# Three transposed contexts read from memory by columns, and the sums of self attention in another buffer

## The chip, the cores and the metric

The kernel runs on one core of one Trainium2 chip. The metric is the device time of one execution in microseconds (us). The core has five engines that run their own instruction streams in order and wait for each other by semaphores: TensorE (PE in the profile, with its weight loads as PEld), VectorE (DVE), ScalarE (ACT), GpSimd (POOL) and SyncE (SP). Transfers between memory and the on-chip buffers are issued by an engine's instruction stream, here SP's or ACT's, and carried out by 16 DMA engines.

## The reference

One decoder layer in fp32 on 4 entries of 512 tokens by 512 features, 16 heads of 32 features:

```python
x = x + self_attention(layernorm(x))      # causal; q, k, v and o projections with biases
x = x + cross_attention(layernorm(x), ctx, ctx)   # no projections; causal, masked scores are -10000
x = x + ffn(layernorm(x))                 # relu(x Wup) Wdown + sum(top-2 softmax) * (x Wexpert)
```

In cross attention the context is both key and value, without a projection. The scores contract over a head's features, so TensorE needs the context with its features on the partitions (512 features as 4 chunks of 128 partitions, by 512 tokens); the values need it with its tokens on the partitions, as it lies in memory.

## The kernel before

The four entries are worked on one after the other, but overlapped: while the engines do the softmax of one stage, TensorE is filled with matmuls of another (the feed-forward of entry b beside the maxima of self attention of entry b+1, for example). The order of PE, DVE, ACT and POOL is written out by hand and is the order of the program text. SP's order is set by the framework. Each engine takes its instructions strictly in that order, the issue of a DMA included.

For each entry b the stages are:

1. maxima of self attention (`with_maxima`): score matmuls (`sm_s`, L286), a copy by ACT (`s_s`, L297), a mask by POOL and a maximum by DVE, with the previous entry's feed-forward or this entry's projections as filler;
2. scores, exponentials and values of self attention (`attend`): `sc_s`, ACT's exponentials, `pv_s`. For the head groups g = 0, 1, 2 the sums of the exponentials are gathered in a buffer `self.sums[g]` of one full activation tile, taken from the buffers `ck_t` (g even) and `beh_t` (g odd);
3. the output projection (`pm_o`, L687). Between its matmuls stand the side steps: the transposes that make the transposed context `ckT` (from `cv`, by `columns`: 8 transposes `tp_c` on PE into PSUM and one copy by ACT, done twice for an entry) and the transposes that make the next entry's `xnT` (`tp_a`). After its second chunk `behind` lets DVE scan `ckT` from the back (L672);
4. query and key projection of the next entry, then maxima (`sm_c`) and `attend` of cross attention, which read `ckT`;
5. value projection of the next entry (`pm_v`), the back transposes `tp_x`, the layernorm, and the transposes `tp_f` with ACT's copy `fT` that open the feed-forward.

All activation tiles have one buffer for each tag, so `ck_t` holds the sums of self attention first and the transposed context after them. `load_cv` reads the context of entry b+1 on SP right after cross attention of entry b, when `cv` is free. `load_x(0)` puts two of its four loads on ACT's queue; all other loads are SP's, until one store at the end.

In the program before, the first entry's ACT instructions are: two loads, the copies of `xnT`, then the query and key outputs `kT` and `qT` (L604, L607).

A DMA of this program carries its completion in one of eight semaphores, given out in rotation over all DMAs in the framework's order. A DMA whose semaphore is still in use by an earlier one waits for that one before it is issued.

Of the kernel before, what the change touches and what calls it, by code (L numbers as in the profile page):

```python
# [9 lines left out]
F32 = mybir.dt.float32  # L10
# [8 lines left out]
P = 128  # L19
# [7 lines left out]
def decoder_layer(  # L27
# [21 lines left out]
    nc = tc.nc  # L49
    B, S, D = x.shape  # L50
# [3 lines left out]
    NC = D // P  # L54
# [5 lines left out]
    act = ctx.enter_context(tc.tile_pool(name="act", bufs=1))  # L60
# [17 lines left out]
    def load_cv(b):  # L78
        cv = act.tile([P, NT, D], F32, tag="cv", name=f"cv_{b}")
        src = ctx_in[b].rearrange("(t p) d -> p t d", p=P)  # L80
        for t in range(NT):
            nc.sync.dma_start(out=cv[:, t, :], in_=src[:, t, :])
        return cv

    def load_w(ap, name, parts=1):
        w = const.tile([P, NC, ap.shape[-1]], F32, tag=name, name=name)
# [175 lines left out]
    class Attention:  # L262
# [114 lines left out]
        def scores(self, pieces):  # L377


            at, N = [], 0  # L380
            for g, j in pieces:
                at.append(N)
                N += S - j * P
            name = f"{self.name}_{pieces[0][0]}_{pieces[0][1]}"
            scs = [pair(f"sc_{name}_{n}") for n in range(2)]
            for (g, j), c in zip(pieces, at):
                for r in range(HG):
                    h = slice(r * HD, (r + 1) * HD)
                    nc.tensor.matmul(  # L389
                        scs[r // 2][:, r % 2, c : c + S - j * P],  # L390
                        lhsT=self.k_t[h, g, j * P : (j + 1) * P],
                        rhs=self.q_t[h, g, j * P :],
                        start=(c == 0),
                        stop=False,
                        skip_group_check=(len(pieces) > 1),
                    )
            for (g, j), c in zip(pieces, at):
                for r in range(HG):
                    h = slice(r * HD, (r + 1) * HD)
                    nc.tensor.matmul(  # L400
                        scs[r // 2][:, r % 2, c : c + S - j * P],
                        lhsT=onesb[h, :],
                        rhs=self.mrow[g][h, j * P :],
                        start=False,
                        stop=True,
                        skip_group_check=(len(pieces) > 1),
                    )
            g, j = pieces[0]
            pts = []
            if j == 0 and g in self.added:  # L410

                self.sums[g] = act.tile(
                    [P, 2, 2, S],
                    F32,
                    tag="v" if self.cross else ("ck_t", "beh_t")[g % 2],
                    name=f"sum_{name}",
                )
            for n in range(2):
                if j == 0 and g in self.added:
                    pt = self.sums[g][:, n]  # L420
                else:
                    pt = work.tile([P, 2, S], F32, tag="pt", name=f"pt_{name}_{n}", bufs=6)
                nc.scalar.activation(pt, scs[n], AF.Exp)  # L423

                if len(pieces) == 1:
                    diagonal = pt[:, :, :P].unsqueeze(2)
                elif j == pieces[1][1]:
                    diagonal = pt.rearrange("p u (k q) -> p u k q", k=2)[:, :, :, :P]
                else:
                    diagonal = pt[:, :, : 2 * P].rearrange("p u (k q) -> p u k q", k=2)  # L430
                nc.gpsimd.affine_select(  # L431
                    out=diagonal,
                    in_=diagonal,
                    compare_op=ALU.is_ge,
                    fill=0.0,
                    base=0,
                    pattern=[[0, 2], [0, len(pieces)], [1, P]],
                    channel_multiplier=-1,
                )
                pts.append(pt)  # L440
            return [(g, j, c, pts) for (g, j), c in zip(pieces, at)]
# [144 lines left out]
    def add_bias(e):  # L586
        for t in range(NT):
            nc.gpsimd.tensor_tensor(e.x[:, t, :], e.x[:, t, :], bo_sb, ALU.add)
# [67 lines left out]
    def context(e):  # L656

        b = e.b
        e.cv = cvs.pop(b)
        e.ck_t = act.tile([P, NC, S], F32, tag="ck_t", name=f"ckT_{b}")  # L660

        def one(t):
            columns([e.cv[:, t, :], e.cv[:, t + 1, :]], e.ck_t, t, pair(f"tp_c{b}_{t}"))

        return [(lambda t=t: one(t)) for t in (0, 2)]
# [15 lines left out]
    def out_projection(e, a, sides):  # L681

        b = e.b
        pms = [pair(f"pm_o{b}_{n}") for n in range(2)]
        for c in range(NC):
            for t in range(NT):
                nc.tensor.matmul(  # L687
                    pms[t // 2][:, t % 2, :],
                    lhsT=a.out[:, c, t * P : (t + 1) * P],
                    rhs=wo_sb[:, c, :],  # L690
                    start=(c == 0),
                    stop=(c == NC - 1),
                )
            if c < NC - 1:
                run(sides[c::3])
            if c == 1:
                for g in range(NC):
                    behind(e, g)

        def add(t):  # L700
            xi = e.x[:, t, :]
            nc.vector.tensor_tensor(xi, pms[t // 2][:, t % 2, :], xi, ALU.add)

        made, norms = layernorms(lambda t: e.x[:, t, :], f"q{b}", add)
        run(norms)
        return made
# [147 lines left out]
    def run(steps):  # L854
        for step in steps:
            for _ in step() or ():
                pass
# [89 lines left out]
    with tc.manual_schedule(engines=BY_HAND):  # L947
        e, norms, turns = norm_in(0, x0)
        keep_warm("warm", 12)
        run(norms)  # L950
        run(turns)
        nc.gpsimd.tensor_scalar(bqs_sb, bq_sb, SCALE, None, ALU.mult)
        nc.vector.tensor_reduce(
            fold, ident.rearrange("p (c e) -> p e c", e=HD), axis=AX.X, op=ALU.add
        )
        add_bias(e)
        between_self = query_key(e) + value(e)
        skip, between_cross, ahead = 4, [], []
        for b in range(B):
            more = b + 1 < B  # L960
            sa = Attention(e.q_t, e.k_t, e.v, False, f"s{b}")
            norms, turns = [], []
            if more:
                after, norms, turns = norm_in(b + 1)
            late = with_maxima(between_self, sa, skip, norms)
            if b == B - 1:
                e.x = load_x(b)
            attend(sa, late)
            if b > 0:
                add_bias(e)  # L970
            made = out_projection(e, sa, context(e) + turns)
            steps = (query_key(after) if more else []) + between_cross
            run(steps[:2])
            norm_cross(e, made, 0)
            run(steps[2:3])
            norm_cross(e, made, 2)
            ca = Attention(e.cq_t, e.ck_t, e.cv, True, f"c{b}")
            ca.e, ca.out = e, e.beh_t
            late = with_maxima(steps[3:], ca)
            if b + 2 < B:  # L980
                after.x = load_x(b + 1)
            attend(ca, late)
            if more:
                cvs[b + 1] = load_cv(b + 1)
            filler = value(after) if more else ahead
            run(filler[:1])
            made = add_cross(e, ca)

            fill = matmuls(filler[1:])
            for t, k in ((0, 8), (2, 2)) if b != B - 2 else ((0, 12), (2, 0)):  # L990
                for _ in range(k):
                    next(fill)
                norm_ffn(e, made, t)
            for _ in fill:
                pass
            gates, ups, downs, experts = ffn(e)
            if b + 3 < B:
                between_self, between_cross = gates[:1] + ups + gates[1:] + downs, experts
            elif b + 2 < B:
                between_self, between_cross = gates[:1] + ups + gates[1:] + downs, []  # L1000
                ahead = experts
            elif more:
                between_self, ahead = ahead + ups[:2], experts
                between_cross = gates[:1] + ups[2:] + gates[1:] + downs
            else:
                run(gates[:1] + ups + gates[1:])
                run(downs[:2] + experts[:2] + downs[2:] + experts[2:])
            skip = 0
            if more:
                e = after  # L1010
# [48 lines left out]
```

## Time and profile before

| | |
|---|---|
| time, median of 3 runs | 809.8 us (809.56 to 809.82) |
| the profiled execution | 809.92 us, of which its span is 808.2 us |
| PE busy | 796.8 us (99% of the span), 5616 matmuls |
| DVE busy | 563.7 us (70%) |
| ACT busy | 395.4 us (49%) |
| POOL busy | 332.8 us (41%) |
| DMA queue of SP (q1) | 13184 packets, 22.96 MB |
| DMA queue of ACT (q10) | 432 packets, 0.66 MB |
| context load `cv` | 16 DMAs of 256 KB, 4.0 us from issue to landing |
| `tp_c` transposes and `ckT` copies | 64 and 8 in four entries |

Busy time counts instructions that compute. Instructions that issue a DMA are not counted as busy, but they appear in the timeline of their engine's queue (ACTq, SPq). A releaser in a row names what ended an engine's idle time before it. The time outside the span (1.7 us) is not resolved by the profile.

### The profile page before, as it was taken

The page shows a single profiled execution, that of the slowest core. Times are in us where ns is not written, and L with a number is a line of the kernel's source. Part 1 is how long each engine was busy: PE and PEld are TensorE (multiplying, and loading weights), DVE is VectorE, ACT ScalarE, POOL GpSimd, SP SyncE. Part 2 cuts the span into 40 slices and gives each one's busy share as a digit, 9 for nine tenths or more (in the row PEclk, how much of TensorE's full clock was granted, in tenths as well). Part 3 has the DMA queues.
Part 4 walks back from the last instruction along what each step waited for, and adds up shares of the span by engine and source line. Part 5 has one row for each costly group of instructions (what it writes and reads, how often), then busy time and mean ns, then how long its engine had stood idle before and what let it go on. Part 6 is the DMA issues. An engine that isn't in the chain of part 4 may idle for free. (4 is left out here: it accounts for less than half of the span.)

```text
span 808.2 us, 13950 instructions
## 1 busy us (share of the span) xinstructions
PE 796.8 (99%) x5616; PEld 379.9 (47%) x5616; DVE 563.7 (70%) x957; ACT 395.4 (49%) x448; POOL 332.8 (41%) x523
## 2 busy tenths in 40 slices
PE   8999999999999999999999999999999999999998
PEld 7444454444444454444544445444444454434444
DVE  2478865879678854588867786688859766988512
ACT  2457526861546515566045752686056824674110
POOL 4334612554234732266333482266423653465100
PEclk9999999999999999999999999999999999999999
DMA  9601000001001000020100000000102000000101
GB/s 337 236 28 28 1 1 1 2 2 53 1 27 27 2 1 0 2 77 29 53 14 14 1 2 1 0 2 1 54 26 79 2 2 0 1 2 2 52 1 52
DMA packets 13680, 24.50 MB, mean 30 GB/s; under 512 B 1968, under 2 KB 2224, under 8 KB 13616
## 3 DMA queue, kind: packets, MB, share of 16 engines
q1 hardware_dynamic: 13184, 22.96, 8.4%
q8 instruction: 44, 0.72, 0.4%
q10 hardware_dynamic: 432, 0.66, 0.2%
q14 instruction: 20, 0.16, 0.1%
HBM read 19.42 MB, written 4.19 MB: 29 GB/s over the span
## 5 line engine op out<-in xcount | busy, mean ns | idle before, releaser
L317 DVE TENSOR_REDUCE nm_s<-s_s 128x2 f32<-128x1024 f32 (+3 forms) x128 | 97.0, 811 | 35.2 <-POOL s_s L305 35.2
L317 DVE TENSOR_REDUCE nm_c<-s_c 128x2 f32<-128x1024 f32 (+3 forms) x128 | 95.8, 810 | 31.0 <-POOL s_c L305 31.0
L297 ACT COPY s_s<-sm_s 128x1024 f32<-128x1024 f32 x80 | 77.1, 1015 | 70.7 <-PE sm_s L286 36.4
L297 ACT COPY s_c<-sm_c 128x1024 f32<-128x1024 f32 x80 | 77.1, 1016 | 35.9 <-PE sm_c L286 16.2
L305 POOL TENSOR_SCALAR_AFFINE_SELECT s_c<-s_c 128x512 f32<-128x512 f32 (+1 forms) x80 | 43.9, 550 | 100.4 <-ACT s_c L297 100.4
L305 POOL TENSOR_SCALAR_AFFINE_SELECT s_s<-s_s 128x512 f32<-128x512 f32 (+1 forms) x80 | 43.8, 551 | 97.1 <-ACT s_s L297 97.1
L423 ACT ACTIVATE pt_c<-sc_c 128x1024 f32<-128x1024 f32 x64 | 61.7, 1031 | 21.0 <-PE sc_c L400 15.4
L510 DVE TENSOR_TENSOR sum_s<-sum_s,pt_s 128x256 f32<-128x256 f32 (+2 forms) x72 | 59.8, 895 | 16.7 <-PE pv_s L462 16.7
L431 POOL TENSOR_SCALAR_AFFINE_SELECT pt_c<-pt_c 128x512 f32<-128x512 f32 (+1 forms) x64 | 51.1, 806 | 27.0 <-ACT pt_c L423 26.6
L223 PE MATMUL pm_d<-wdown_sb,hT 128*128 128x512 f32 x128 | 61.5, 610 | 0.0
L423 ACT ACTIVATE pt_s<-sc_s 128x1024 f32<-128x1024 f32 x56 | 53.9, 1030 | 12.6 <-PE sc_s L400 7.0
L235 PE MATMUL pm_u<-fT,wup_sb 128*128 128x512 f32 x128 | 59.3, 604 | 0.0
L223 PE MATMUL pm_v<-wv_sb,xnT 128*128 128x512 f32 x128 | 58.8, 600 | 0.0
L687 PE MATMUL pm_o<-wo_sb,oT_s 128*128 128x512 f32 x128 | 57.8, 596 | 0.0
L235 PE MATMUL pm_qk<-xnT,wk_sb 128*128 128x512 f32 x120 | 57.3, 607 | 0.0
L389 PE MATMUL sc_c<-cqT,ckT 32*128 32x384 f32 (+3 forms) x512 | 56.0, 464 | 1.4 <-ACT sum_c L423 0.8
L235 PE MATMUL pm_qk<-xnT,wq_sb 128*128 128x512 f32 x120 | 56.7, 604 | 0.0
L223 PE MATMUL pm_e<-wexp_sb,fT 128*128 128x512 f32 x120 | 56.3, 604 | 0.0
L389 PE MATMUL sc_s<-qT,kT 32*128 32x128 f32 (+3 forms) x512 | 54.4, 462 | 1.2 <-ACT sum_s L423 0.9
L431 POOL TENSOR_SCALAR_AFFINE_SELECT pt_s<-pt_s 128x512 f32<-128x512 f32 (+1 forms) x56 | 48.1, 868 | 17.6 <-ACT pt_s L423 17.0
L286 PE MATMUL sm_c<-ckT,cqT 32*128 32x512 f32 (+3 forms) x512 | 47.5, 460 | 0.0
L286 PE MATMUL sm_s<-kT,qT 32*128 32x512 f32 (+3 forms) x512 | 47.0, 461 | 0.0
(164 smaller groups left out, 1269.3 us busy)
## 6 DMA issues: line engine op xcount, KB each, us to landing
cv<-in_ctx_dram SPq DMA_DIRECT2D x16, 256.0 KB, 4.0
out_dram<-x SPq DMA_DIRECT2D x15, 256.0 KB, 2.0
x<-in_x_dram SPq DMA_DIRECT2D x14, 256.0 KB, 4.1
xin<-in_x_dram SPq DMA_DIRECT2D x12, 256.0 KB, 2.7
wq_sb<-in_wq_dram SPq DMA_DIRECT2D x2, 512.0 KB, 6.2
wk_sb<-in_wk_dram SPq DMA_DIRECT2D x2, 512.0 KB, 7.8
wv_sb<-in_wv_dram SPq DMA_DIRECT2D x1, 1024.0 KB, 8.3
wo_sb<-in_wo_dram SPq DMA_DIRECT2D x1, 1024.0 KB, 9.7
```

What stands on the lines that cost most here:

```text
L223: nc.tensor.matmul(pm, lhsT=lhs_t[:, c, t * P : (t + 1) * P], rhs=w[:, c, :], start=(c == 0), stop=(c == NC - 1),)
L235: nc.tensor.matmul(pm, lhsT=w[:, c, f * P : (f + 1) * P], rhs=rhs_t[:, c, :], start=(c == 0), stop=(c == NC - 1),)
L286: nc.tensor.matmul(scs[r // 2][:, r % 2, c : c + (i + 1) * P], lhsT=self.q_t[h, g, i * P : (i + 1) * P], rhs=self.k_t[h, g, : (i + 1) * P] ...
L297: nc.scalar.copy(s, scs[n])
L305: nc.gpsimd.affine_select(out=diagonal, in_=diagonal, compare_op=ALU.is_ge, fill=NEG, base=0, pattern=[[0, 2], [0, len(pieces)], [-1, P]], ...
L317: nc.vector.tensor_reduce(self.nm[g][:, i, 2 * n : 2 * n + 2], made[n][:, :, c : c + (i + 1) * P], axis=AX.X, op=ALU.max, negate=True,)
L389: nc.tensor.matmul(scs[r // 2][:, r % 2, c : c + S - j * P], lhsT=self.k_t[h, g, j * P : (j + 1) * P], rhs=self.q_t[h, g, j * P :], start= ...
L423: nc.scalar.activation(pt, scs[n], AF.Exp)
L431: nc.gpsimd.affine_select(out=diagonal, in_=diagonal, compare_op=ALU.is_ge, fill=0.0, base=0, pattern=[[0, 2], [0, len(pieces)], [1, P]], ...
L510: nc.vector.tensor_tensor(to, to, pts[n][:, :, c : c + S - j * P], ALU.add)
L687: nc.tensor.matmul(pms[t // 2][:, t % 2, :], lhsT=a.out[:, c, t * P : (t + 1) * P], rhs=wo_sb[:, c, :], start=(c == 0), stop=(c == NC - 1),)
```

## The change

For the entries 0, 1 and 2, `ckT` is no longer made by TensorE from `cv`. A new function `load_turned` reads the context from memory with a rearranged access pattern: for each of four chunks of 128 features, one DMA of 256 KB from ACT's queue, whose partition is the feature and whose inner direction is the token, so that neighbours in the tile are 2048 bytes apart in memory. Entry 3 keeps the transposes. The load for entry 0 stands after the first `xnT` copies; those of entries 1 and 2 stand after cross attention of the entry before. So that `ck_t` is free from the end of cross attention on, the even sums of self attention go to the buffer of `xn_t`, except in entry 3. The side steps of the output projection are dealt out anew, because there are two fewer.

```diff
+    def load_turned(b):
+        t = act.tile([P, NC, S], F32, tag="ck_t", name=f"ckT_{b}")
+        src = ctx_in[b].rearrange("s (c p) -> c p s", p=P)
+        for c in range(NC):
+            nc.scalar.dma_start(out=t[:, c, :], in_=src[c])
+        return t
...
+                even = "xn_t" if self.name != f"s{B - 1}" else "ck_t"
                 self.sums[g] = act.tile(
                     [P, 2, 2, S],
                     F32,
-                    tag="v" if self.cross else ("ck_t", "beh_t")[g % 2],
+                    tag="v" if self.cross else (even, "beh_t")[g % 2],
...
         e.cv = cvs.pop(b)
+        if b < B - 1:
+            e.ck_t = turned.pop(b)
+            return []
         e.ck_t = act.tile([P, NC, S], F32, tag="ck_t", name=f"ckT_{b}")
...
             if c < NC - 1:
-                run(sides[c::3])
+                run(sides[c::3] if b == B - 1 else sides[c // 2 : c // 2 + 1][: 1 - c % 2])
...
+        turned = {0: load_turned(0)}
         add_bias(e)
...
             if more:
                 cvs[b + 1] = load_cv(b + 1)
+            if b + 2 < B:
+                turned[b + 1] = load_turned(b + 1)
```

## The prediction

> **What bounds the kernel now.** I read the page's engine rows first, then its DMA queues, then the timelines of SP, ACT and PE around the places where the new loads stand.
>
> ```profile
> PE 796.8 (99%) x5616; PEld 379.9 (47%) x5616; DVE 563.7 (70%) x957; ACT 395.4 (49%) x448; POOL 332.8 (41%) x523
> PEclk9999999999999999999999999999999999999999
> q1 hardware_dynamic: 13184, 22.96, 8.4%
> q10 hardware_dynamic: 432, 0.66, 0.2%
> ```
>
> PE is busy for 99% of the span at full granted clock, so PE work removed is time won, and anything that makes PE stop is time lost at once. The DMA engines are nearly idle on average (8.4%), but their queues matter here for the engine that issues.
>
> SP's issues at the start (start, duration of the issue, tile):
>
> ```profile
> 14.37 0.38 SPq L90 DMA_DIRECT2D wup_sb<-in_wup_dram  x1
> 15.08 0.37 SPq L90 DMA_DIRECT2D wdown_sb<-in_wdown_dram  x1
> 15.80 2.01 SPq L120 DMA_DIRECT2D wgate_sb<-in_wgate_dram  x1
> 17.85 3.45 SPq L90 DMA_DIRECT2D wexp_sb<-in_wexp_dram  x1
> 21.34 3.07 SPq L568 DMA_DIRECT2D xin<-in_x_dram  x2
> ```
>
> `wup`, `wdown`, `wgate` and `wexp` each have 512 pieces, 32 for each of 16 DMA engines, plus one for the semaphore. Two take 0.37 us to issue, the next two 2.01 and 3.45 us. Counting pieces issued against the trace's packet records, each engine has 104 pieces outstanding when `wup` is issued, 128 after `wdown`, and 129 after `wgate`; none of these counts goes higher. So an issue runs freely up to about 128 pieces for each DMA engine; from there the issuing engine is held until old pieces have gone.
>
> ACT and PE after cross attention of entry 0:
>
> ```profile
> 184.15 1.94 ACT L423 ACTIVATE pt_c<-sc_c 128x1024 f32<-128x1024 f32 x2 [0.53 <-issue]
> 203.18 1.01 ACT L257 COPY fT<-tp_f 128x1024 f32<-128x1024 f32 x1 [17.08 <-PE tp_f L251]
> 205.77 1.01 ACT L257 COPY fT<-tp_f 128x1024 f32<-128x1024 f32 x1 [1.58 <-PE tp_f L251]
> ```
>
> ```profile
> 207.38 1.15 PE L286 MATMUL sm_s<-kT,qT 32*128 32x256 f32 x16
> 208.46 1.06 PE L759 MATMUL lg<-fT,wgate_sb 128*32 128x512 f32 x8
> ```
>
> ACT has 17.1 us without work (186.1 to 203.2); then PE needs `fT` at 208.5. Entry 1 has the same pattern (last exponential ends at 384.0, `fT` at 401.1). In entry 0 the new load comes here:
>
> ```profile
> 11.79 1.01 ACT L257 COPY xnT<-tp_a 128x1024 f32<-128x1024 f32 x1 [0.75 <-PE tp_a L251]
> 18.70 0.69 ACT L604 ACTIVATE kT<-pm_qk,bk_sb 128x512 f32<-128x512 f32 x1 [5.90 <-PE pm_qk L622]
> ```
>
> **What the change removes.** In three entries 16 `tp_c` transposes each: a group of 8 moves PE on by 0.88 us (`tp_c` at 100.22, `tp_a` at 101.09), so 1.76 us an entry, 5.3 us together, all on PE's path. Six ACT copies of 1.01 us and DVE's 8.2 us wait for `ckT` go too; they lie beside PE work and count nothing.
>
> **What it moves at no cost.** The even sums in `xn_t`: its readers `pm_qk` and `pm_v` stand before the scores on PE, so ACT's first exponential waits for nothing new. The next `xnT` needs `sum_s` read: the last reader (`ls_s`, 93.99 us) stands ahead of `pm_o` (96.68) on PE, so PE's order hides it; without that order, a copy of 1.0 us would wait. The new places of `tp_a` among `pm_o` keep 3.6 us of `pm_o` matmuls behind each step.
>
> **What it adds.** Twelve loads on ACT's queue. Neighbours in the tile are 2048 bytes apart in memory, so each element is a piece: 128x512 = 65,536 pieces a DMA, 4096 for each DMA engine, and 16,388 for an entry with semaphores. No piece of 4 bytes from memory is in the trace (the 4-byte packets are semaphores). The nearest row is `wgate`: 512 pieces of 32 bytes, each 9 ns long in the packet records, and following one another every 5.9 ns on one engine (the first 18 start 5 to 6 ns apart). `bk` and `bq` (16 bytes) keep the same step. At 5.9 ns an entry is 16,388 x 5.9 = 96.7 us of all 16 engines, against about 2.7 us as plain rows.
>
> Here a rule of the Trainium skill is to be weighed. "DMA: Bandwidth & Descriptors", section "Rules for kernel authors", speaks against this change: a strided last dimension becomes one descriptor for each element, and a transpose by a rearranged access pattern is 19 times slower than the hardware's DMA transpose. With the page's 261 GB/s for the latter ("Latency and other measured facts"), 1.05 MB would take, as an estimate, 1.05/(261/19) = 76 us an entry. The same page's small-transfer row gives 10.5 ns a packet ("Bandwidth"): 172 us an entry. The trace's row lies between, and I take it: 96.7. With the rule my sum would be 3 x 20 = 61 us less. Both ends stay for the range. A slower step is the likelier error: `wgate` reads 16 KB in one place, queued behind other traffic so its reads could run ahead, while the new loads stride over 1 MB.
>
> **Who waits.** ACT issues, and by the 128-piece limit it is held until all but 128 pieces of the fourth DMA are taken: 96.7 - 0.8 = 95.9 us. Behind it in ACT's order stand:
>
> Entry 0: ACT reaches the load at 12.8 us. The DMA engines then still have work of SP until 32.8 us (the windows of 1 us show a DMA share near 1 until there), 20 us; about 2 us of it, three loads of x, come behind the new loads on reused semaphores. The engines share their time, so ACT is free at 12.8 + 18 + 95.9 = 126.7. Then `kT`, `qT`, `kT`, `qT` take 2.6 us, and `sm_s`, before at 27.2, starts at 129.3: 102.1 us. PE can't go past `sm_s`, since its order is fixed.
>
> Entries 1 and 2: issue from 186.1, about 1.5 us until pieces move (a lone `xin` lands in 2.7 us, 0.7 of it data), 2.9 us for SP's `cv` load beside it, 95.9 of pieces: ACT is free at 286.4. Two `fT` copies, then `lg` at 288.4 rather than 208.5: 79.9 us. PE's `pm_v` and `sm_s` are done meanwhile; four PSUM pairs leave it nothing else. The same for entry 2. SP's later loads that reuse a semaphore of the new loads, and `cv` and the stores that share the engines with them, are late by less than ACT is held, so I count nothing; without that hold they would count (rival C).
>
> After each stop PE may start slowly: the trace's first 28 warming matmuls took 5.22 us against 0.109 us each later, 2.1 us more. I count it three times, 6.3 us (bounds: nothing, and 13 if twice that).
>
> Sum: 102.1 + 2 x 79.9 - 5.3 + 6.3 = 262.9. The profiled execution is 809.9 us (808.2 of span and 1.7 around it), 0.1 over the median: 809.9 + 262.9 = 1072.8, or 1073.
>
> **Rivals.** A, as above with a step of 4.6 to 7 ns: 1000 to 1130 us, chance 0.60.
>
> B, held, but small strided reads are slower: at 10.5 ns each entry gains 16,388 x 4.6 = 75 us, 1299 us. For: the new reads jump. Against: `wgate`'s step. Chance 0.24 up to 10.5 ns, and 0.04 beyond.
>
> C, ACT isn't held (the queue takes a DMA as a whole). Then SP still waits: in the built order `x` loads on SP's queue wait for semaphores of the new loads, and the third `xin` stands behind them. It would land near 12.8 + 18 + 96.7 + 5 = 133 us, against its statistics on DVE at 52.25: some 78 us less a little slack, all in entry 0; later loads have time. 810 + 78 - 5 = 883. Against it: SP's 2.01 and 3.45 us. Chance 0.07.
>
> D, faster: the pieces are joined, or pass so quickly that a load fits in ACT's pause. The place is the 17.1 us pause; with the 3.3 us by which ACT can trail (`lg` at 208.5), the hold may last about 20 us, 1.2 ns a piece. Below that the loads after cross attention cost nothing; joined fully, as fast as `cv`'s 4.0 us, only the 5.3 us of transposes count: 805. For: the DMA engines are idle there. Against: the 5.9 ns step for 16 and 32 bytes. Chance 0.05, of which 0.01 ends within 0.2%.
>
> **How the numbers follow.** The likeliest case gives 1073. The range runs from 1000 (the 76 us estimate gives 1012, less the warming twice) to 1300 (10.5 ns); it leaves out C, D and the end of B, 0.16. About 0.2% is what a measurement of this kernel can tell from no change; faster by more 0.04, within it 0.01, slower 0.95.
>
> **What would show it.** In the profile after: q10 with about 790,000 packets; ACT's queue with four issues of over 20 us each, three times; gaps of some 100, 80 and 80 us in PE's timeline, from about 27, 310 (208.5 + 102.1) and 588 us (406.5 + 182) on; `tp_c` 16 instead of 64. I am wrong if ACT's issues are short (C, D), if their length over 4096 isn't near 5.9 ns (B), or if PE's gaps don't begin where ACT is held.

## The result: 1149.7 us against 809.7, and the profile after

The changed kernel takes 1149.71 us (median of 4 runs, 1149.4 to 1151.14) against 809.73 us before: a ratio of 1.420, 95% interval 1.418 to 1.422. The prediction was 1073, with a range of 1000 to 1300. The profiled execution took 1151.14 us, its span 1148.3 us, 340.1 us more than the span before.

The page of the changed kernel: engine rows, PE's busy tenths and granted clock in 40 slices of 28.7 us, and the queue of ACT (packets, MB, share of 16 engines).

```profile
PE 801.6 (70%) x5568; PEld 378.1 (33%) x5568; DVE 570.0 (50%) x957; ACT 389.5 (34%) x442; POOL 338.2 (29%) x523
PE   8000084999991003999999500099999999999998
PEclk9555587999996556999999855599999999999999
q10 hardware_dynamic: 787056, 3.80, 67.8%
...
ckT<-in_ctx_dram ACTq DMA_DIRECT2D x12, 256.0 KB, 81.4
```

PE has about as much to do as before (801.6 us against 796.8), but is idle for 30% of the span, mostly in three places. ACT's queue now carries 787,056 packets, nearly all of them single elements. A load takes 81.4 us from issue to landing in the median, where `cv` took 4.0; about half of that is spent before the queue takes it.

ACT's timeline in the first two places, the rows of its queue among those of its computing (start, duration, what, idle time before it):

```profile
11.84 134.28 ACTq L90 DMA_DIRECT2D ckT<-in_ctx_dram  x4
146.23 0.69 ACT L613 ACTIVATE kT<-pm_qk,bk_sb 128x512 f32<-128x512 f32 x1 [133.68 <-issue]
...
327.08 0.67 ACTq L90 DMA_DIRECT2D ckT<-in_ctx_dram  x1
327.47 1.01 ACT L432 ACTIVATE pt_c<-sc_c 128x1024 f32<-128x1024 f32 x1
327.79 120.01 ACTq L90 DMA_DIRECT2D ckT<-in_ctx_dram  x3
447.84 1.93 ACT L265 COPY fT<-tp_f 128x1024 f32<-128x1024 f32 x2 [119.36 <-issue]
```

ACT is held in the issue of its loads: 134.3 us in entry 0, then 0.67 us for the first load of entry 1 and 120.0 us for the other three. Entry 2 repeats entry 1 (0.64 and 120.13 us). SP, on its own queue, is not held meanwhile: it issues four loads of `cv` in 3.2 us.

```profile
331.44 3.21 SPq L82 DMA_DIRECT2D cv<-in_ctx_dram  x4
```

What that cost PE is in the table of waits (waiting engine and line, who ended the wait, us in total, times, longest):

```profile
PE sm_s L294 <- ACT fT L265: 198.0, 2, 99.1
...
PE sm_s L294 <- ACT qT L616: 120.6, 1, 120.6
...
PE sm_s L294 <- DVE v L656: 17.0, 1, 17.0
```

One stop of 120.6 us for entry 0's load, two of 99 us for the others, and a fourth of 17.0 us at 182 us, which is not ACT's. DVE and SP show where the fourth comes from:

```profile
194.31 0.69 DVE L202 BATCH_NORM_STATS2 st_a<-xin 128x6 f32<-128x512 f32 x1 [19.31 <-DMA xin<-in_x_dram]
```

```profile
148.84 40.80 SPq L75 DMA_DIRECT2D x<-in_x_dram  x4
189.75 24.03 SPq L577 DMA_DIRECT2D xin<-in_x_dram  x4
```

```profile
SPq L75 <- DMA ckT<-in_ctx_dram: 78.1, 2, 39.2
```

DVE waits for the third `xin`. SP couldn't issue it sooner, because it stood behind the four loads of x. By the last row, two of those waited for semaphores of transposed loads, 39 us each: the second x until the fourth transposed load landed at 188 us, 42 us after ACT had been released.

The sum: 120.6 + 17.0 + 198.0 = 335.6 us of stops, less 5.3 us of transposes, makes 330.3 of the 340.1. Most of the other 9.8 us is PE's clock, and PE's busy time shows it: 801.6 us is 10.1 more than 796.8 less the transposes. Windows around the end of the second stop (span and length, busy us and instructions of each engine, then the granted clock, the DMA share and GB/s):

```profile
446.00:448.00 2.00, 0.00 (x0) 0.00 (x0) 0.00 (x0) 0.16 (x1) 0.00 (x0) 0.50 1.77 6
448.00:450.00 2.00, 1.10 (x12) 0.95 (x16) 0.00 (x0) 1.76 (x2) 0.00 (x0) 0.50 0.53 3
450.00:452.00 2.00, 2.00 (x20) 0.47 (x12) 0.00 (x0) 0.97 (x2) 0.00 (x0) 0.50 0.84 6
452.00:454.00 2.00, 2.00 (x9) 0.68 (x4) 1.22 (x3) 1.44 (x3) 1.27 (x2) 0.93 1.16 8
454.00:458.00 4.00, 4.00 (x24) 1.97 (x23) 2.56 (x6) 1.93 (x2) 0.93 (x2) 1.00 1.67 8
```

PE resumes at 448.9 us with half the clock and has all of it again from about 452 us on, which costs 1.6 us. The same windows around the others give 2.2, 3.6 (half the clock from 199.2 to about 206.5 us) and 1.7: some 9 us together.

### The profile page after: what moved, and what is told of

Its sections match the earlier page's. It is cut to its first block, busy times and chain, and to the rows that moved or that the text cites. A ratio compares the mean times of both kernels' runs of the same rounds, so it can differ in the third digit from the quotient of the medians.

```text
span 1148.3 us, 13871 instructions
## 1 busy us (share of the span) xinstructions
PE 801.6 (70%) x5568; PEld 378.1 (33%) x5568; DVE 570.0 (50%) x957; ACT 389.5 (34%) x442; POOL 338.2 (29%) x523
## 3 DMA queue, kind: packets, MB, share of 16 engines
q10 hardware_dynamic: 787056, 3.80, 67.8%
## 5 line engine op out<-in xcount | busy, mean ns | idle before, releaser
L294 PE MATMUL sm_s<-kT,qT 32*128 32x512 f32 (+3 forms) x512 | 52.0, 494 | 335.5 <-ACT fT L265 198.0
L294 PEld LDWEIGHTS sm_s<-kT,qT 32*128 32x128 f32 x512 | 25.5, 199 | 370.8 <-ACT fT L265 199.6
L325 DVE TENSOR_REDUCE nm_c<-s_c 128x2 f32<-128x1024 f32 (+3 forms) x128 | 95.9, 811 | 31.0 <-POOL s_c L313 31.0
L265 ACT COPY fT<-tp_f 128x1024 f32<-128x1024 f32 x8 | 7.8, 1014 | 277.7 <-issue 238.5
L613 ACT ACTIVATE kT<-pm_qk,bk_sb 128x512 f32<-128x512 f32 x16 | 11.0, 688 | 164.1 <-issue 133.7
L231 PE MATMUL pm_v<-wv_sb,xnT 128*128 128x512 f32 x128 | 61.4, 622 | 0.0
## 6 DMA issues: line engine op xcount, KB each, us to landing
ckT<-in_ctx_dram ACTq DMA_DIRECT2D x12, 256.0 KB, 81.4
```

The costliest lines, as they stand in the source:

```text
L231: nc.tensor.matmul(pm, lhsT=lhs_t[:, c, t * P : (t + 1) * P], rhs=w[:, c, :], start=(c == 0), stop=(c == NC - 1),)
L294: nc.tensor.matmul(scs[r // 2][:, r % 2, c : c + (i + 1) * P], lhsT=self.q_t[h, g, i * P : (i + 1) * P], rhs=self.k_t[h, g, : (i + 1) * P] ...
L325: nc.vector.tensor_reduce(self.nm[g][:, i, 2 * n : 2 * n + 2], made[n][:, :, c : c + (i + 1) * P], axis=AX.X, op=ALU.max, negate=True,)
```

## The experiments

Two questions were open: what holds ACT, and why a piece takes longer than 5.9 ns. For the first, theory 1 is that a queue takes a DMA whole and holds the engine at the next one; theory 2 is the prediction's, that the engine is held by everything over 128 pieces for each DMA engine.

**How much of the load is held: one DMA, and two.** The tile is laid out token by token, so that a whole entry is one regular row of steps of 512 bytes and can be one DMA or two. TensorE then reads it with a step of 16 bytes.

```diff
-        for c in range(NC):
-            nc.scalar.dma_start(out=t[:, c, :], in_=src[c])
+        flat, src = t.rearrange("p s c -> p (s c)"), ctx_in[b].rearrange("s (c p) -> p (s c)", p=P)
+        for n in range(1):                       # 2 in the second kernel
+            part = slice(n * 2048, (n + 1) * 2048)  # 1024
+            nc.scalar.dma_start(out=flat[:, part], in_=src[:, part])
+        return t.rearrange("p s c -> p c s")
```

> Each entry's transposed load is one DMA of the same 262,144 pieces (tile laid out token by token, four chunks side by side, so TensorE and VectorE read it with a step of 16 bytes; source step 512 bytes). Theory 1 (a queue takes one DMA whole and holds the engine at the next one until the first has been taken): ACT's three issues last under 1 us each, no hold. The data is then late: entry 0 lands near 185 us and the x load and third xin on SP's queue wait for its semaphore, so TensorE loses about 134 us there; entries 1 and 2 land about 155 us after issue, 35 us after the scans want them. 1000 to 1030 us. Theory 2 (the prediction's: held until all but 128 pieces per DMA engine are taken): each issue lasts some 150 us and the time is over 1200 us.

> As the one-DMA kernel, but in two DMAs of 131,072 pieces. Theory 1: first issue under 1 us, second about half of the load's time (77 us; entry 0 some 95 us with SP's traffic beside it): TensorE loses about 57 us in each of entries 1 and 2, and in entry 0 still about 134 us by the late xin. About 1050 us. Theory 2: both issues together some 150 us, over 1200 us.

Measured: 1085.72 and 1103.3 us. The issues of the transposed load, from the one-DMA kernel and then from the two-DMA kernel (count, then ns of the shortest, median and longest):

```profile
L91 ACTq DMA_DIRECT2D ckT<-in_ctx_dram x3: 636/636/736, 12.2 to 595.2; - x3
```

```profile
L91 ACTq DMA_DIRECT2D ckT<-in_ctx_dram x6: 636/40440/91060, 11.7 to 604.9; - x6
```

A DMA of 262,144 pieces, 16,385 for each engine, is issued in 0.64 us when nothing is before it in the queue. With two, the second takes 80 us (91 in entry 0). So a DMA's own pieces don't hold the engine: the queue took each of these whole, and the next issue waited until the one before was all or nearly all done. Of N equal loads N - 1 were held. Theory 1 stands, and the prediction's rule falls as far as a DMA's own pieces go.

How nearly done isn't settled. In entry 1 of the changed kernel (ns of the shortest, median and longest issue; then us from issue to landing):

```profile
L90 ACTq DMA_DIRECT2D ckT<-in_ctx_dram x4: 667/38728/42468, 327.1 to 408.9; - x4
DMA to landing us min/median/max: 44.9/81.0/83.8
```

The second issue ends at 327.8 + 42.5 = 370.3 us, 1.7 us before the first load lands (327.1 + 44.9). SP's small DMAs in the profile before did stand behind each other, up to 128 pieces an engine. A rule that lets in the next DMA, whole, once no more than about that many pieces are left fits both; no run here tests it.

Both times lie over 50 us above what was expected. PE is busy for 833.4 and 838.1 us here, some 32 and 37 us more than in the changed kernel: it reads the step of 16 bytes more slowly, shown below. The late data also cost more than the 35 us expected, 50 us in each of entries 1 and 2 of the one-DMA kernel (1 MB lands after 161.3 us, and DVE waits 62.0 us for it). Its stops:

```profile
PE sm_s L295 <- DVE v L657: 137.2, 1, 137.2
PE tp_q L260 <- DVE xn_q L215: 101.6, 4, 50.2
```

**The moved sums alone.**

```diff
-                    tag="v" if self.cross else ("ck_t", "beh_t")[g % 2],
+                    tag="v" if self.cross else (("xn_t" if self.name != f"s{B - 1}" else "ck_t"), "beh_t")[g % 2],
```

> The kernel before, with only the even sums of self attention moved to the buffer of xn_t (entries 0 to 2); all contexts are transposed by TensorE. If the move costs nothing, as predicted: within 0.2% of before, 809.8 us. If a wait came with it (xnT waiting for the sums, or a feed-forward tile waiting for the buffer): slower by 1 us or more for each entry.

Measured: 809.71 us, ratio 0.9999 (0.9990 to 1.0008). The move costs nothing.

**Whether the jump in memory makes the piece slow.**

```diff
-        src = ctx_in[b].rearrange("s (c p) -> c p s", p=P)
+        src = ctx_in[b].rearrange("s d -> (s d)").rearrange("(h p s u) -> h u p s", h=2, p=P, u=2)
...
-            nc.scalar.dma_start(out=t[:, c, :], in_=src[c])
+            nc.scalar.dma_start(out=t[:, c, :], in_=src[c // 2, c % 2])
```

> The changed kernel with the same number of 4-byte pieces in the same DMAs, read with a step of 8 bytes instead of 2048 (other elements of the context, so the values of cross attention are not the reference's). If the jump in memory is what makes a piece take more than 5.9 ns: issues of about 24 us and a time near 1000 us. If a 4-byte piece costs the same wherever it is read: issues of 38 to 39 us, as in the changed kernel, and about 1150 us.

Measured: 1185.16 us. The held issues take 41 to 52 us, against 38.6 to 49.3 in the changed kernel. Reading nearby doesn't help; it is slower by some 10%. So the jump, which the prediction feared, isn't the price.

**What a piece costs.**

```diff
+        runs = ctx_in[b].rearrange("s d -> (s d)").rearrange("(h p s v u) -> h v p s u", h=2, p=P, v=2, u=8)
...
+            if b == 1:
+                for part in (slice(0, 116), slice(116, P)):
+                    nc.scalar.dma_start(out=t[part, c, :], in_=src[c][part])
+            elif b == 2:                    # runs: pieces of 8 elements, every second one
+                dst = t[:, c, :].rearrange("p (s u) -> p s u", u=8)
+                nc.scalar.dma_start(out=dst, in_=runs[c // 2, c % 2])
+            else:
                 nc.scalar.dma_start(out=t[:, c, :], in_=src[c])
```

> The changed kernel with other pieces in two entries, to time a piece. Entry 0 as in the changed kernel. Entry 1: each chunk as a DMA of 116 features and one of 12, so that the large one is shared by 4 DMA engines (14,848 pieces of 4 bytes each) and the small one by 12. Entry 2: pieces of 32 bytes with a step of 64 bytes, 512 for each engine in a DMA (other elements of the context, so the values of cross attention in entry 2 are not the reference's). If a piece costs an engine 9.4 ns whatever the others do: entry 1's large DMAs last about 140 us each, entry 2's 4.8 us. If 16 engines together are limited (1.7 pieces a ns) and one alone does a piece in 5.9 ns: large DMAs of about 88 us, entry 2's 3 to 5 us. If only pieces of 4 bytes are slow: entry 2's 3.0 us, 5.9 ns a piece, and 140 us in entry 1.

Measured: 1337.43 us, in a single run; what counts here is the pace of the pieces. Packets in a stretch of 20 us, first of the changed kernel (380 to 400 us, 16 DMA engines at work), then of this one (480 to 500 us, entry 1, four engines at work):

```profile
DMA packets 33997, 0.14 MB, mean 7 GB/s; under 512 B 33997, under 2 KB 33997, under 8 KB 33997
```

```profile
DMA packets 12377, 0.05 MB, mean 2 GB/s; under 512 B 12377, under 2 KB 12377, under 8 KB 12377
```

33,997 pieces in 20 us are 1.70 a ns together, 9.4 ns for each of 16 engines. 12,377, in the middle of a large DMA, are 6.5 ns for each of four. (The count of ACT's queue, 557,680 packets, leaves 16 packets for the semaphores of each pair of DMAs, as 4 and 12 engines would send.) ACT's issues in entry 1 agree:

```profile
L93 ACTq DMA_DIRECT2D ckT<-in_ctx_dram x8: 1295/50642/101911, 326.0 to 639.7; - x8
```

Behind the large DMAs they are held for 95 to 102 us; for 14,848 pieces that is 6.4 to 6.9 ns each. It is more than the 88 us expected and far from 140. So a piece costs an engine less when only four work, and in a long run 16 together are limited.

For a moment, though, 16 engines go as fast. The changed kernel in entry 1, just after the loads of `cv` have passed (340 to 342 us, in 40 slices):

```profile
GB/s 9 10 10 10 10 11 11 11 11 11 11 11 11 11 11 11 10 10 10 9 9 8 9 8 7 8 7 7 7 7 7 7 7 6 7 6 6 6 6 6
```

The first microsecond has 2595 packets, 6.2 ns for each of 16 engines; after the second the pace is 9.4 ns again. Pieces that stood ready behind the other traffic, and then ran out, would explain it; no run here tests that. Nor do the runs separate what sets the pace of the long run: the supply of pieces by the queue, the memory or the buffers.

Pieces of 32 bytes come hardly faster: of entry 2's three held issues one stood beside the loads of `cv`, and the other two took some 4.4 us for 512 pieces an engine, 8.5 ns each.

**Who issues.** The twelve loads from SP.

```diff
-            nc.scalar.dma_start(out=t[:, c, :], in_=src[c])
+            nc.sync.dma_start(out=t[:, c, :], in_=src[c])
```

> The changed kernel with the twelve transposed loads issued by SP instead of ACT. Theory 1 (the issuing engine is held): ACT isn't held any more and SP is, so the loss moves to what SP issues behind: in entry 0 xin and x behind the fourth load (near 160 us, TensorE stops about 110 to 140 us at the statistics of the first xin), in entries 1 and 2 the xin of the next entry and cv wait behind, so a smaller loss than 99 us each, some 40 to 90. 950 to 1120 us. If the loss came from the DMA engines' load and not from who issues: about 1150 us again.

Measured: 1178.8 us, slower than from ACT and above the range expected. SP's timeline:

```profile
329.22 118.42 SPq L90 DMA_DIRECT2D ckT<-in_ctx_dram  x4
447.69 40.25 SPq L82 DMA_DIRECT2D cv<-in_ctx_dram  x4
488.04 6.24 SPq L577 DMA_DIRECT2D xin<-in_x_dram  x2
```

PE's stops:

```profile
PE sm_s L294 <- DVE x L817: 220.8, 2, 110.4
PE sm_s L294 <- ACT s_s L305: 142.9, 1, 142.9
```

The hold moves to SP, as theory 1 says, but the size was misjudged. `cv` stands behind the loads and waits another 40 us for their semaphores, and `xin` stands behind `cv`; its statistics on DVE, which stand in front of the maxima, stop PE for 110.4 us in each of entries 1 and 2, and for 142.9 us in entry 0. Which engine issues decides whose work waits, not whether it does.

**Entry 0 alone.**

```diff
-        if b < B - 1:
+        if b == 0:
             e.ck_t = turned.pop(b)
             return []
...
-            if b + 2 < B:
-                turned[b + 1] = load_turned(b + 1)
```

> The transposed load by columns for entry 0 only; entries 1 to 3 are transposed by TensorE. If the losses are separate, as the trace of the changed kernel has them (120.6 and 17.1 us at entry 0, less 1.7 of transposes): 809.7 + 136 = 946 us. If part of entry 0's loss comes from later loads or the slower clock carries on: more than 3 us off.

Measured: 951.15 us, 5 more than expected. PE's two stops are 120.0 and 17.7 us; with 1.7 us less of transposes this gives 945.7. The same two stops cost the changed kernel 5.8 us by the lower clock after them, which the expected 946 left out and which accounts for the rest. So the losses are separate.

**A version that keeps the gain, first try.** Two buffers for the transposed context, TensorE's transposes for entry 0, and single loads spread over the entry before.

```diff
-        t = act.tile([P, NC, S], F32, tag="ck_t", name=f"ckT_{b}")
+        t = act.tile([P, NC, S], F32, tag=f"ck_{b % 2}", name=f"ckT_{b}")
...
+            turned[b + 1], chunk = load_turned(b + 1)     # chunk(c) issues one DMA
+            chunk(0)
             late = with_maxima(between_self, sa, skip, norms)
+            chunk(1)
...
+            chunk(2)
             ca = Attention(e.cq_t, e.ck_t, e.cv, True, f"c{b}")
...
             late = with_maxima(steps[3:], ca)
+            chunk(3)
```

> A version meant to keep only the gain: two buffers for the transposed context (the small tiles rest and rden with two buffers to make room), entry 0 transposed by TensorE, and the context of entry b+1 loaded by columns during entry b, one DMA of 65,536 pieces at each of four places on ACT's queue (before the maxima of self attention, before its scores, before and after the maxima of cross attention), some 45 us or more apart, more than the 40 us that one takes. Theory 1: no issue is held, the data is there long before it is wanted, and only 3 x 1.75 us of transposes on TensorE are left to gain: 804.4 us. If SP's loads wait for reused semaphores or the slow pieces hinder other transfers: at or above 810. If ACT is held by any piece over 128 (theory 2): four times about 38 us in each entry, over 1150.

Measured: 852.46 us, ratio 1.053 (1.051 to 1.054). Rows of ACT's and of SP's timeline:

```profile
152.40 0.65 ACTq L91 DMA_DIRECT2D ckT<-in_ctx_dram  x1
183.39 9.40 ACTq L91 DMA_DIRECT2D ckT<-in_ctx_dram  x1
```

```profile
22.67 3.36 SPq L579 DMA_DIRECT2D xin<-in_x_dram  x2
70.03 1.75 SPq L75 DMA_DIRECT2D x<-in_x_dram  x4
```

Most issues are short, so theory 2 is out again, but the two waits found above come back. The fourth place is 31 us after the third, less than a load takes, and is held for 9.4 us; that happens in two entries, for nearly 8 us of PE each. And a load of x waits from 26 to 70 us for the semaphore of the first transposed load, with the third `xin` behind it: 21.6 us of PE. The slower clock after the stops makes most of the rest: PE is busy for 802.9 us, 11 more than without the transposes of three entries.

**Second try.** The same with the places moved.

```diff
+            chunk(3)                                      # of this entry's context
             late = with_maxima(between_self, sa, skip, norms)
+            turned[b + 1], chunk = load_turned(b + 1)
+            chunk(0)
...
             made = out_projection(e, sa, context(e) + turns)
+            chunk(1)
...
             late = with_maxima(steps[3:], ca)
+            chunk(2)
```

> As the spaced version, with the four places moved so that they are 40 us or more apart and none stands ahead of the first entry's loads of x and xin: before the scores of self attention, after the output projection, before the scores of cross attention, and at the start of the next entry's maxima. Theory 1: no issue over 1 us, no wait of SP for a transposed load's semaphore, so the 38 us that the spaced version lost to those go, and the transposes' 5.3 us are gained: 804 to 806 us. If the slow pieces themselves cost the other engines or transfers something while they run (some 480 us of the span): 810 us or more with no stop to be seen.

Measured: 804.6 us, ratio 0.9935 (0.9921 to 0.9948): faster than both kernels. The page's engine row, and the twelve issues:

```profile
PE 791.1 (99%) x5568; PEld 374.4 (47%) x5568; DVE 573.4 (71%) x957; ACT 389.5 (49%) x442; POOL 341.0 (42%) x523
```

```profile
L91 ACTq DMA_DIRECT2D ckT<-in_ctx_dram x12: 635/636/737, 66.5 to 586.0; - x12
```

No issue is held. PE does 5.7 us less than before, and the span, 802.7 us, is 5.5 us shorter. SP still waits twice for the semaphore of a transposed load (13.9 us for a `cv`, 13.3 us for an x), which had not been expected, but at places where nothing stops for it. The DMA engines handle the same 787,056 packets of ACT's queue, now behind a PE that is busy for 99% of the span.

## Why the prediction held, and where its sum was wrong

The bound (PE stops at once when ACT is late), the place of the three large stops, their order of size and the fate of the transposes and sums were right. PE stops before `sm_s` in entry 0, as the text said. In entries 1 and 2 it also stops before `sm_s`, waiting for ACT's `fT`; the text had that `sm_s` done meanwhile and the stop at `lg`, one step later. The transposes were sized right: in entry 0 PE takes 15.6 us from the first `pm_o` to `pm_qk` where it took 17.3, 1.75 us less for each entry. The slow start, counted at 6.3 us, was about 9, as there was a fourth stop.

Three terms of the sum were wrong, all in "What it adds" and "Who waits":

- **The piece: 5.9 ns expected, 9.4 to 9.8 measured over an entry.** The row chosen, `wgate`, was a burst of 32 pieces for an engine, behind other traffic. Sixteen engines reach 6.2 ns in a burst of the changed kernel too, but not in a long run, and the trace of before had no long run. The prediction saw that this error would be the likelier one (rival B) and gave two reasons: the jump in memory, though a step of 8 bytes was no faster than one of 2048, and that `wgate`'s reads could run ahead behind other traffic, which fits the burst.
- **The hold: all but 128 pieces expected, all but the last DMA measured.** The 128 pieces in SP's rows of before are real, but they are the place where many small DMAs stopped, not a limit inside one. At 9.8 ns the prediction's rule would have given 160 us an entry; three loads of four are 120. Of the signs it named, four long issues an entry were three.
- **The fourth stop, 17.0 us.** Rival C named its mechanism, x behind the semaphore of the new loads and the third `xin` behind x, but only as an alternative to the hold. The text counted SP's late loads at nothing, since ACT would be held longer. As the fourth load is not held, ACT is free 42 us before it lands, and that cover was gone.

The first two errors lie in opposite directions: 95.9 us of hold expected, 120.7 measured in entries 1 and 2, which makes their stops 99 rather than 79.9 us, and entry 0's 120.6 rather than 102.1. Together: 18.5 + 2 x 19.1 + 17.0 + 3 = 76.7 of the 77 us between forecast and result.

That the result lies in the range, and within 8% of the forecast, is partly luck. As estimates from the measured terms: with the piece alone put right, the sum would have been some 1265 us (three entries at 160.6 rather than 96.7); with the hold alone (three quarters of 96.7) and the 17.0 us, about 1020. The likeliest case, rival A, ended at 1130; the measured pace is one that the text gave to rival B, with a chance of 0.24.

The rule of the Trainium skill ("DMA: Bandwidth & Descriptors", "Rules for kernel authors": 19 times slower than the hardware's transpose, an estimate of 76 us an entry) pointed the right way, but the measurement decides: the one DMA with an entry's pieces landed after 161 us. The same page's 10.5 ns a packet ("Bandwidth") made an estimate of 172 us and lies nearer. That may be chance: the page gives it for the 64 packets of one small transfer issued from GpSimd, and doesn't say that it is the pace of a single DMA engine, as the prediction took it.

## What to carry to other kernels

A transfer with one piece for each element costs by the number of pieces, 40 us for 256 KB here, and can still be worth it where the DMA engines are idle and the bound engine is relieved. What decides is the engine that issues: here one long DMA was taken at once, and a second behind it held the whole instruction stream, so spread them at least one transfer's time apart in the order of the issuing engine, and follow which later loads reuse their semaphores. When a duration comes from a burst, ask whether a long run with all engines at work would keep that pace.

## What the hardware showed that was not expected

TensorE's moving operand read with a step of 16 bytes is slower. The maxima of cross attention, in the changed kernel and then in the one-DMA kernel (three of whose four entries read that layout; us in total, mean ns of one):

```profile
L294 PE MATMUL sm_c<-ckT,cqT 32*128 32x512 f32 x128 | 19.2, 640 | 0.0
```

```profile
L295 PE MATMUL sm_c<-ckT,cqT 32*128 32x512 f32 x128 | 30.3, 989 | 0.0
```

The weights that are read with that step, in `sc_c`, load more slowly too (184 ns in the median before, 304 then).

VectorE's scan over the context, 1.2 us each before, takes up to 2.2 us where it no longer waits for ACT's copy. In the fastest version it then runs beside GpSimd's addition of the bias, and both are longer than when they ran one after the other. Their timelines there:

```profile
283.37 7.77 DVE L686 TENSOR_TENSOR_SCAN behT<-ckT,zero 128x511 f32<-128x511 f32 x4
```

```profile
282.37 7.69 POOL L599 TENSOR_TENSOR x<-x,bo_sb 128x512 f32<-128x512 f32 x4
```

Before, the four scans took 4.56 us and the four additions 4.97. That the two engines hinder each other is read from the timelines; no run took one of them away. It cost nothing here: the scans still end before PE has finished `pm_o`.
